# First-layer decays issued in mid-step through a spare PSUM bank, scans reordered; taps, squares and weight buffers changed in the third layer

## The chip, the core and the metric

The kernel runs on one core of a Trainium2 chip. Five engines work from their own queues, each in order: TensorE (PE, with its weight loads shown apart as PEld), VectorE (DVE), ScalarE (ACT), GpSimd (POOL) and SyncE (SP), which here issues all DMAs. The metric is the device time of one execution in microseconds (us), lower is better; the median of three runs of the kernel before is 7789.27 us.

## What is computed

A batch of 8 images of 384 channels and 32 x 32 pixels goes through four residual layers, each of the form `x = x + layer(group_norm(x))`, all in float32. Layers 0 and 2 are selective scans over the 1024 pixels of an image, with 768 inner channels `d` and 16 states `n` each; layer 2 adds a layer norm ahead of it and an MLP behind it. Layer 1 is a 1x1 convolution, an 8x8 patch filter in the frequency domain, a 3x3 depthwise convolution and a gate. Layer 3 is a 3x3 depthwise convolution. The core of layers 0 and 2:

```
def step(h, inp):
    dt_t, B_t, C_t, u_t = inp
    dA = jnp.exp(dt_t[..., None] * A)
    h = dA * h + (dt_t * u_t)[..., None] * B_t[:, None, :]
    y = jnp.einsum('bdn,bn->bd', h, C_t)
    return (h, y)
...
y = jnp.swapaxes(ys, 0, 1) + u * D
y = y * jax.nn.silu(z)
return y @ out_proj_w.T
```

## The kernel before, in words

**Tiling.** Each of the two scan layers is cut into 16 chunks (8 images, two halves of T = 512 pixels). A chunk is 24 steps (`QUADS`: six blocks of 128 inner channels, four sub-blocks each), so the main loop (lines 1015 to 1045) has 768 steps `t`. A step covers 32 inner channels x 16 states as four tiles of 128 x 512, j = 0 to 3. Steps 0 to 383 are layer 0 and steps 384 to 767 are layer 2.

**One step.** `begin` (line 610) loads dt*u for the step, repeated over the states, into a tile `g` (four tiles wide, four buffers), three steps ahead. `times` (line 619) multiplies `g` by B on POOL, two instructions of 128 x 1024, for step t+1. `decay` (line 627) spreads dt over the states by four matmuls of 32 rows into four PSUM banks `dAs[0..3]`, and ACT takes the exponentials in place. `scan` (line 637) runs four DVE scans, j = 0, 1, 2, 3. For j = 0 and 1 the result goes back into the bank and DVE multiplies it by C into `g` (line 654). For j = 2 and 3 it goes into `g`, and POOL multiplies both by C in one instruction (line 660). In the first half of an image, DVE copies keep the last column as `carry`. `gather` (line 664) sums over the states by matmuls into a bank `y`, one step later. At the end of a block of 128 channels it adds u*D (in layer 0 with a diagonal matrix `w_D`, loaded at the start by `load_diagonal`; in layer 2 on DVE) and multiplies by silu(z).

**Order.** It is written out by hand: the order of the calls is the order in each engine's queue. In the loop: `times(t+1)`, `scan(t)`, some job work (`jobs.step(t, 2.0)`, up to about 2 us of TensorE work), `gather(t-1)`, `begin(t+3)`, the rest of the job work (`jobs.step(t)`), and last `decay(t+1)`. In this text the two portions of job work are called J1 and J2.

**Jobs.** All else is cut into pieces by generators, and `Jobs` (line 90 on) puts them into the steps: `front` (loads, norms, input projection, the dt tiles), `gates` (z), `finish` (output projection; the MLP in layer 2), `layer1`, `layer3` and `measure` (group statistics). Each step grants a room of TensorE and DVE work (`ROOM`: 5.2 and 3.0 in layer 0, 6.4 and 3.0 in layer 2). Jobs go by due time, and `jobs.until` runs them at once where the loop can't go on without them. So work that was put off comes in a burst inside one step.

**PSUM.** Eight banks: four for the decays, one for `y`, and three (`NBANK`) that all jobs share in turn through `ps_tile` (line 179) and `pipe` (line 189). `live["ps"]` counts those in use; a job that finds none yields `WAIT`.

**The other places that the change touches.** `step_dt` (line 566) makes one dt tile per block: softplus with a scratch tile `spm` (two buffers, which `measure` and `layer_norm` use too, guarded by the flag `live["spm"]`), then dt*u into its own tile `du` (two buffers), which is spilled to DRAM. `layer_norm` (line 460, layer 2) squares a 128 x 512 tile on ACT and sums it on PE, three times in turn, through two buffers. `depthwise` (line 364) makes a diagonal matrix per tap on ACT and accumulates nine matmuls per tile; `layer3` (line 970) calls it for six tiles of 128 x 512 per image, then adds x on DVE into a single buffer `acc` and writes it out. `weights` (line 873) streams the MLP's weights from DRAM in pieces of 384 KB through four buffers `mw`.

```
        jobs.begin(ROOM["turn" if n == B * NCH else s["pre"]])
        jobs.step(t, 2.0)
        if t > 0:
            p, q = steps[t - 1]
            gather(p, q)
...
            begin(p, q)
        jobs.step(t)
        if t + 1 < total:
            decay(*steps[t + 1])
```

## Time and profile before

| what | value |
|---|---|
| median of 3 runs | 7789.27 us (7788.77 to 7790.12) |
| profiled execution, own time | 7774.96 us |
| its span on the core | 7773.2 us |
| mean granted TensorE clock | 0.922 of full speed |
| first scan starts at | 95.1 us |
| layer 0, steps 0 to 383 | 95.1 to 3552.3 us, 9.00 us a step |
| chunks 16 and 17 (the turn to layer 2) | 3552.3 to 4123.8 us |
| chunks 18 to 31 (layer 2, 336 steps) | 4123.8 to 7587.8 us, 10.31 us a step |
| tail after the last scan | 7587.8 to 7773.2 us |

Busy times are unions of the instructions' spans. A line of a group reads: source line, engine, operation, output<-inputs, shape, count | busy us, mean ns of one | idle time of that engine just before them, with what ended it. Helpers record for many callers: line 177 is every matmul, line 241 every activation, line 85 every metered DVE operation. A float32 matmul appears as two records, so the counts of PE are twice those of the program. In the timeline a line has the start, the duration, the engine and the instructions merged into it, with the idle time before the first of them in brackets.

### The profile page before, as it was taken

To read this page: it belongs to the slowest core of one execution; us is meant where nothing else is said; L and a number is where in the kernel's file an instruction comes from. 1 tells how busy PE (TensorE), PEld (TensorE's weight loads), DVE (VectorE), ACT (ScalarE), POOL (GpSimd) and SP (SyncE) were. 2 spreads that over 40 slices of the span, in tenths; PEclk is the share of its full clock that TensorE was granted. 3 is DMA by queue.
4 is the path that set the end of the run, shared out by engine and by line. 5 is a ranking of instruction groups with operands and counts; after the bars stand their busy time and mean duration, and the time that the engine had idled before them with its cause. 6 is when DMAs were issued, how large, how long until landed. Compare 5 with 4: busy or idle time off the path is not lost. (4 is left out here: it accounts for less than half of the span.)

```text
span 7773.2 us, 76689 instructions
## 1 busy us (share of the span) xinstructions
PE 7244.1 (93%) x25762; PEld 3001.0 (39%) x25762; DVE 5787.0 (74%) x7350; ACT 4034.0 (52%) x6980; POOL 5638.8 (73%) x2710
## 2 busy tenths in 40 slices
PE   7989999999999999999999989999999999999998
PEld 2223333333333333333334434444444444444445
DVE  5988788888777878778746765767777677776871
ACT  4445555554554555455545544555555555555543
POOL 5888878788787878778646764767767677676770
PEclk8888889999888999988899999999999999999999
DMA  5666556556565646556536654666656666565662
GB/s 141 141 151 144 138 134 142 136 135 150 127 146 127 141 120 148 128 139 146 129 78 167 174 135 120 165 156 172 165 150 174 155 170 164 149 164 146 171 168 67
DMA packets 288919, 1122.50 MB, mean 144 GB/s; under 512 B 37386, under 2 KB 90970, under 8 KB 190220
## 3 DMA queue, kind: packets, MB, share of 16 engines
q1 hardware_dynamic: 288524, 1117.59, 58.4%
q8 instruction: 204, 3.34, 0.2%
q14 instruction: 191, 1.56, 0.1%
HBM read 1041.96 MB, written 75.50 MB: 144 GB/s over the span
## 5 line engine op out<-in xcount | busy, mean ns | idle before, releaser
L623 POOL TENSOR_TENSOR g<-g,bc 128x1024 f32<-128x1024 f32 x1536 | 3586.8, 2358 | 197.2 <-DMA g<-dud 181.2
L660 POOL TENSOR_TENSOR g<-g,bc 128x1024 f32<-128x1024 f32 x768 | 1806.2, 2352 | 1441.1 <-DVE carry L656 806.6
L241 ACT ACTIVATE dA<-dA,w_A 128x512 f32<-128x512 f32 x3072 | 1860.7, 662 | 1543.3 <-PE dA L177 1530.1
L177 PE MATMUL dA<-dt,selr 32*128 32x512 f32 x6144 | 1573.3, 677 | 70.6 <-DVE g L654 61.9
L643 DVE TENSOR_TENSOR_SCAN dA<-dA,carry,g 128x512 f32<-128x512 f32 x768 | 986.6, 1285 | 616.0 <-issue 275.6
L643 DVE TENSOR_TENSOR_SCAN dA<-dA,g 128x512 f32<-128x512 f32 x768 | 940.6, 1225 | 477.5 <-issue 167.7
L654 DVE TENSOR_TENSOR g<-dA,bc 128x512 f32<-128x512 f32 x1536 | 1053.9, 686 | 29.8 <-DVE dA L643 0.5
L177 PE MATMUL y<-g,sely 128*32 128x512 f32 x6144 | 934.1, 637 | 43.0 <-POOL g L660 37.5
L643 DVE TENSOR_TENSOR_SCAN g<-dA,carry,g 128x512 f32<-128x512 f32 x768 | 940.6, 1267 | 0.0
L643 DVE TENSOR_TENSOR_SCAN g<-dA,g 128x512 f32<-128x512 f32 x768 | 893.3, 1204 | 0.0
L177 PEld LDWEIGHTS dA<-dt,selr 32*128 32x128 f32 x6144 | 470.2, 191 | 984.4 <-DVE g L643 517.3
L177 PE MATMUL ps_dn<-h,mw 128*128 128x256 f32 x2304 | 573.9, 401 | 75.3 <-DMA mw<-in_l_mlp_w 58.6
L177 PE MATMUL ps_up<-t,mw 128*128 128x256 f32 x2304 | 566.8, 394 | 59.0 <-DMA mw<-in_l_mlp_w 44.2
L177 PE MATMUL ps_z<-xf,w_in 128*128 128x512 f32 x1152 | 586.1, 649 | 27.3 <-DVE dt L85 23.6
L177 PE MATMUL ps_in<-xf,w_in 128*128 128x512 f32 x1152 | 566.9, 633 | 27.3 <-DVE u L85 25.5
L177 PE MATMUL ps_dw<-tp,diag 96*96 96x512 f32 x1152 | 572.8, 638 | 15.2 <-ACT diag L241 15.2
L177 PE MATMUL ps_out<-u,w_out 128*128 128x512 f32 x1152 | 543.7, 619 | 10.2 <-DVE x L85 10.2
L177 PEld LDWEIGHTS ps_dn<-h,mw 128*128 128x128 f32 x2304 | 439.5, 197 | 277.0 <-issue 118.8
L177 PEld LDWEIGHTS ps_up<-t,mw 128*128 128x128 f32 x2304 | 425.8, 192 | 268.4 <-issue 148.9
L177 PE MATMUL ps_dw<-xp,diag 128*128 128x512 f32 x864 | 407.5, 622 | 42.2 <-ACT diag L241 40.9
L241 ACT ACTIVATE u<-ps_in,w_vec 128x512 f32<-128x512 f32 x192 | 149.4, 778 | 484.2 <-PE ps_in L177 484.2
L177 PEld LDWEIGHTS y<-g,sely 128*32 128x32 f32 x6144 | 134.2, 111 | 648.5 <-issue 461.1
(99 smaller groups left out, 6463.1 us busy)
## 6 DMA issues: line engine op xcount, KB each, us to landing
g<-dud SPq DMA_DIRECT2D x768, 1024.0 KB, 7.1
mw<-in_l_mlp_w SPq DMA_DIRECT2D x384, 384.0 KB, 7.4
dud<-du SPq DMA_DIRECT2D x768, 64.0 KB, 1.7
xk<-in_x SPq DMA_DIRECT2D x48, 256.0 KB, 4.2
xf<-in_x SPq DMA_DIRECT2D x16, 768.0 KB, 8.4
x<-in_x SPq DMA_DIRECT2D x16, 768.0 KB, 8.5
x_mid<-x SPq DMA_DIRECT2D x16, 768.0 KB, 4.6
xk<-x_mid SPq DMA_DIRECT2D x48, 256.0 KB, 5.0
```

The lines of the kernel that those rows point to most:

```text
L177: nc.tensor.matmul(out_, lhsT, rhs, start=start, stop=stop)
L241: nc.scalar.activation(out_, in_, func, **kw)
L623: nc.gpsimd.tensor_mul(g, g, s["bc"][:, 0, :].unsqueeze(1).to_broadcast([P, 2, T]))
L643: nc.vector.tensor_tensor_scan(dAs[j] if j < own else g[:, j, :], dAs[j], g[:, j, :], 0.0 if s["c"] == 0 else carry[:, q : q + 1], ALU.mul ...
L654: nc.vector.tensor_mul(g[:, j, :], dAs[j], s["bc"][:, 1, :])
L660: nc.gpsimd.tensor_mul(g, g, s["bc"][:, 1, :].unsqueeze(1).to_broadcast([P, 4 - own, T]))
```

## The change

**In layer 0** the four scans of a step go in the order 2, 3, 0, 1 (`ORDER`), and POOL's multiplication of tiles 2 and 3 by C is queued once they are done. `decay(t+1)` moves ahead of J2, and its exponentials are issued in the order 2, 3, 0. The fourth (j = 1, `decay_last`) stays behind J2 and is written into another bank, `b2`, which the jobs therefore lose while layer 0 runs: they have two banks, and get `b2` back after the last scan of layer 0. The diagonal of D is made by ACT from the identity, block by block, instead of loaded.

**In layer 2** the order of scans and exponentials is 2, 3, 0, 1 as well; all four exponentials stay in place, and `decay(t+1)` stays at the end of the step. Everywhere `times` multiplies the upper half of `g` first.

**In layers 2 and 3**, three of the nine taps of layer 3 go from TensorE to POOL: per tile three multiplications by a per-channel weight (`tap`) and three additions (`acc`, beginning with x), and the DVE addition takes `acc` for x. `layer_norm` makes all three squares first, in three buffers, then the three matmuls. MLP weights have five buffers for four. `spm` has three buffers for two and also takes dt*u (`du` is gone), and its flag now tells who holds it.

```
+OWN = 2
+ORDER = (2, 3, 0, 1)
...
-    psg = ctx.enter_context(tc.tile_pool(name="psg", bufs=NBANK, space=PSUM))
+    psg = ctx.enter_context(tc.tile_pool(name="psg", bufs=1, space=PSUM))
...
+    live = {"dt": 0, "x": 0, "spm": None, "banks": ["b0", "b1"]}
...
+    def bank(name):
+        tag = live["banks"].pop(0)
+        ps = psg.tile([P, 512], F32, tag=tag, name=name)
+        held[id(ps)] = ps, tag
+        return ps
+    def ps_done(ps):
+        live["banks"].append(held.pop(id(ps))[1])
...
         while live["spm"]:
             yield WAIT
+        live["spm"] = "squares"
+        sq = [wk.tile([P, T], F32, tag="spm", name="sq", bufs=3) for _ in range(KC)]
+        for k in range(KC):
+            act(sq[k], xn[:, k, :], AF.Square)
+        yield NEXT
         ps = yield from ps_tile("ps_lv")
         for k in range(KC):
-            sq = wk.tile([P, T], F32, tag="spm", name="sq", bufs=2)
-            act(sq, xn[:, k, :], AF.Square)
-            mm(ps, ln_mean, sq, start=k == 0, stop=k == KC - 1)
+            mm(ps, ln_mean, sq[k], start=k == 0, stop=k == KC - 1)
...
-                v = got["du"] = wk.tile([P, T], F32, tag="du", name="du", bufs=2)
-                nc.gpsimd.tensor_mul(v, s["dt"][d], u[d])
+                nc.gpsimd.tensor_mul(got["m"], s["dt"][d], u[d])
...
-        for j in (0, 2):
+        for j in (2, 0):
             g = s["g", i][:, j : j + 2, :]
...
     def decay(s, i):
         k, sub = QUADS[i]
         for j in range(4):
             rows = slice(32 * j, 32 * (j + 1))
             mm(dAs[j], selr[rows, sub, :], s["dt"][k][rows, :])
...
-        for j in range(4):
-            act(dAs[j], dAs[j], AF.Exp, scale=s["w"]["A"][:, 4 * i + j : 4 * i + j + 1])
+        s["dA"] = list(dAs)
+        for j in ORDER:
+            if j != ORDER[-1] or s["pre"] == "l2_":
+                act(dAs[j], dAs[j], AF.Exp, scale=s["w"]["A"][:, 4 * i + j : 4 * i + j + 1])
+
+    def decay_last(s, i):
+        if s["pre"] == "l0_":
+            j = ORDER[-1]
+            s["dA"][j] = psg.tile([P, T], F32, tag="b2", name="dAx")
+            act(s["dA"][j], dAs[j], AF.Exp, scale=s["w"]["A"][:, 4 * i + j : 4 * i + j + 1])
...
+        dA = s["dA"]
-        for j in range(4):
+        for j in ORDER:
...
+            elif j == 3:
+                if s["c"] < NCH - 1:
+                    nc.vector.tensor_copy(
+                        carry[:, 4 * i + OWN : 4 * i + 4].unsqueeze(2), g[:, OWN:4, T - 1 : T]
+                    )
+                r = g[:, OWN:4, :]
+                nc.gpsimd.tensor_mul(
+                    r, r, s["bc"][:, 1, :].unsqueeze(1).to_broadcast([P, 4 - OWN, T])
+                )
...
+        if sub == NSUB - 2 and s["pre"] == "l0_":
+            s["D", k] = wk.tile([P, P], F32, tag="D", name="D")
+            act(s["D", k], eye, AF.Copy, scale=s["w"]["vec"][:, k, 4:5])
...
-                w = p2.tile([P, NFH, P], F32, tag="mw", name="mw", bufs=4)
+                w = p2.tile([P, NFH, P], F32, tag="mw", name="mw", bufs=5)
...
+                acc = p2.tile([P, T], F32, tag="acc", name="acc")
+                so_far = x[hf][:, k, :]
+                for t in range(3):
+                    tap = p2.tile([P, T], F32, tag="tap", name="tap")
+                    nc.gpsimd.tensor_scalar_mul(_img(tap), window(0, t), dw3[:, k, t : t + 1])
+                    nc.gpsimd.tensor_add(acc, tap, so_far)
+                    so_far = acc
+
                 def take(ps):
-                    acc = p2.tile([P, T], F32, tag="acc", name="acc")
-                    vector.tensor_add(acc, ps, x[hf][:, k, :])
+                    vector.tensor_add(acc, ps, acc)
                     nc.sync.dma_start(out[b, k * P : (k + 1) * P, rows], acc)

-                yield from depthwise(p2, P, [(dw3[:, k, :], window, take)])
+                yield from depthwise(p2, P, [(dw3[:, k, :], window, take)], 3)
...
         scan(s, i)
+        if t == total // 2 - 1:
+            live["banks"].append("b2")
         jobs.begin(ROOM["turn" if n == B * NCH else s["pre"]])
         jobs.step(t, 2.0)
...
+        nxt = steps[t + 1] if t + 1 < total else None
+        if nxt and nxt[0]["pre"] == "l0_":
+            decay(*nxt)
         jobs.step(t)
-        if t + 1 < total:
-            decay(*steps[t + 1])
+        if nxt and nxt[0]["pre"] == "l2_":
+            decay(*nxt)
+        if nxt:
+            decay_last(*nxt)
```

## The prediction

> **What bounds the kernel now.** I read the page first, then the busy times by stage, then groups by form, then the timeline. The page says that TensorE is the fullest engine, but not at full clock.
>
> ```profile
> PE 7244.1 (93%) x25762; PEld 3001.0 (39%) x25762; DVE 5787.0 (74%) x7350; ACT 4034.0 (52%) x6980; POOL 5638.8 (73%) x2710
> PEclk8888889999888999988899999999999999999999
> ```
>
> By stage (length; busy PE, PEld, DVE, ACT, POOL; clock), layer 0, then layer 2:
>
> ```profile
> 95.10:3552.30 3457.20, 3265.68 (x10785) 1132.42 (x10786) 2839.63 (x3567) 1816.76 (x3220) 2814.81 (x1349) 0.90 0.58 138
> ...
> 4123.80:7587.80 3464.00, 3225.17 (x12705) 1547.98 (x12704) 2540.83 (x3249) 1841.81 (x3050) 2455.78 (x1174) 0.96 0.63 160
> ```
>
> Layer 0 takes 9.00 us a step; DVE works 2839.6/384 = 7.39 of it and POOL 7.33. DVE's idle 617.6 us is what there is to win. The timeline of one step shows how it arises:
>
> ```profile
> 2021.09 2.45 DVE L643 TENSOR_TENSOR_SCAN g<-dA,carry,g 128x512 f32<-128x512 f32 x2
> ...
> 2023.32 2.84 PE L177 MATMUL ps_out<-u,w_out 128*128 128x512 f32 x6
> ...
> 2026.09 1.14 PE L177 MATMUL dA<-dt,selr 32*128 32x512 f32 x8
> ...
> 2027.25 2.40 ACT L241 ACTIVATE dA<-dA,w_A 128x512 f32<-128x512 f32 x4 [4.22 <-PE dA L177]
> ...
> 2028.00 1.29 DVE L643 TENSOR_TENSOR_SCAN dA<-dA,carry,g 128x512 f32<-128x512 f32 x1 [4.46 <-POOL g L660]
> ```
>
> DVE is done with the scans at E = 2023.54. PE is still on a job matmul and reaches the decays at P = 2026.09. The next scan starts at 2028.00, P + 1.91. (The bracket names POOL, but the first exponential, ending at 2027.9, is what came last.) I took P, E and the next start S from the trace for every step. S - P is never under 1.91. In layer 0, 182 steps have S - P below 1.97, so the arrival of the decays set them: 312 us of DVE idle. The other scan starts lost 106 us and the rest of DVE about 200. In 245 of 384 steps PE came before E and waited for the last scan. So the ring DVE - PE - ACT sets layer 0, with job work of uneven size in it. In layer 2, 228 of 383 steps are set by the decays (548 us); there TensorE's work is the bound.
>
> **What the Trainium skill says.** TensorE: Matmul & The Clock Gate, Part 2, LDWEIGHTS step: matmuls stay in program order, only weight loads are pulled ahead. The trace agrees: the decays above started only after `ps_out`. The same page, Part 1: the clock is full or half, by how busy TensorE was. The trace agrees with 0.43 us against 0.86 from one weight load of `ps_z` to the next, and 0.90 granted in layer 0. GPSIMD Engine Reference, 3.1: an operation with one input can reach 1.8 cycles an element, 769 ns for 512; no run here shows one. For two inputs the trace has 1272 ns (`du`).
>
> **The change part by part.** Prices, with layer norm and weight waits:
>
> ```profile
> L177 PE MATMUL ps_lv<-sq,ln_mean 128*128 128x512 f32 x96 | 72.4, 915 | 40.2 <-ACT sq L241 40.2
> L177 PE MATMUL ps_ln<-xf,ln_mean 128*128 128x512 f32 x96 | 55.6, 725 | 7.9 <-ACT gnm L241 5.7 <-ACT xf L241 2.2
> L177 PE MATMUL ps_dn<-h,mw 128*128 128x256 f32 x2304 | 573.9, 401 | 75.3 <-DMA mw<-in_l_mlp_w 58.6 <-ACT h L241 11.2 <-DVE dA L643 2.6
> L177 PE MATMUL ps_up<-t,mw 128*128 128x256 f32 x2304 | 566.8, 394 | 59.0 <-DMA mw<-in_l_mlp_w 44.2 <-DVE dt L85 5.5 <-ACT h L241 5.4
> L583 POOL TENSOR_TENSOR du<-dt,u 128x512 f32<-128x512 f32 x192 | 244.2, 1272 | 157.2 <-DVE dt L85 153.0 <-DMA dud<-du 4.2
> L241 ACT ACTIVATE diag<-eye,vec 128x128 f32<-128x128 f32 x432 | 160.0, 400 | 161.0 <-PE ps_dw L177 160.7
> ```
>
> (1) Layer 0, ring. In the new order the decays wait for tile 0's multiplication; only scan and multiplication of tile 1 are still to come then, 1.24 + 0.69 = 1.93 us on DVE. Decay to scan is 1.91, so the next scan can follow at once even if PE waited. PE leaves the decays 1.93 us earlier in the step, and is as much earlier at the next ones. Cutting each of the 182 gaps by at most 1.93 removes about 220 us of 312. Of the 106 us others, where POOL's factors were often late, I take 25: POOL starts on tiles 2 and 3 before the last two scans and is some 4 us earlier. I count 200 + 25 = -225. Both ends: 0 if another wait takes over, -365 if DVE idle falls to 250.
>
> (2) Against it, in layer 0. J2 now lies behind the decays, so DVE jobs fed by J2 may arrive after E. The built order has 58 such steps; from the end of the decays (1.1 us of matmuls and 0.3 of handing over), J2's matmuls at 0.43 a record, less the 1.93 and other DVE work, they sum to +45. Two banks: matmuls whose bank was evicted after less than 1 us of other PE work rise from 5 to 55 for ACT (0.6 us eviction) and from 0 to 24 for DVE. ACT: 50 x 0.4 = 20; DVE: 24 x 1 = 24, half hidden by the slack that (1) leaves; +35. Moved past J2 on ACT are three exponentials, 2.0 us; J2's evictions wait for matmuls behind the decays anyway: 0. The fourth exponential waits for the end of tile 1's multiplication, with J1's evictions of the next step queued behind it; it takes 0.66 and is needed 2.45 + 1.93 = 4.4 us into the next step: 0, and 0.7 a step if not. SP: `begin` stays ahead of the decays. D's diagonals: 96 x 400 ns = 38 us of ACT, 53% busy, at least a step ahead: 0, or 38 uncovered. Layer 0: -225 + 80 = -145.
>
> (3) Layer 2, taps. TensorE loses 144 matmuls, 3 x 2 x 0.43 = 2.57 us for each of 48 tiles. POOL gains 3 x (0.8 + 1.27) = 6.2 us a tile, 7.6 if the one-input operation costs as much as the two-input one; I take the page's. In the built order 25 tiles stand alone in a step, 17 in six bursts, 6 in the tail. Alone: 25 x 2.57 = 64, of which 60% (228 of 383) lies on the path: -38. POOL's addition waits for `acc` to be written out (2.0 us to landing), and C's and B's factors queue behind it: 1.5 us for gather or scan, 25 x 1.5 = +38 (0 to 7.6 each). In the bursts a tile is now addition 1.27, two pairs 4.1, DVE 0.7, DMA 2.0 and hand-overs, 8.4 us, where nine taps took 7.7: 0. Tail: 6 x 1 = +6.
>
> (4) Squares: `ps_lv` occupies 112.6 us where the equal `ps_ln` occupies 63.5; 49 x 0.6 = -29. Weights: waits of 58.6 + 44.2 = 103; a fifth buffer takes a third, x 0.6 = -21 (0 to -62).
>
> (5) Layer 2, order of scans with the decays at the end. The last bank free is now tile 1's, second of the four matmuls, with tile 2's exponential behind it; so a scan starts no sooner than E + 1.9, where before it could follow E. Where PE waited (171 steps), filling S - E up to 1.9 gives 82 us; 70%: +57 (0 to 100). The earlier POOL gives -30 of the 116 us that the other scan starts lost. The change in burst sizes at the turn (PE work between decays 103 and 56 us before, 98 and 43 after): -18.
>
> Sum: -145 - 38 + 38 + 6 - 29 - 21 + 57 - 30 - 18 = -180. Profiled execution 7774.96 - 180 = 7595. The median of the runs is 14.3 us above it, so 7609: **7610 us**, 0.977 of before.
>
> **Rivals.** *The ring opens fully in layer 0*: DVE idle there falls to 250. For it: PE's own need is only 5.36 us between decays (built order, 0.43 a record) + 1.07 for the decays at full clock, under DVE's 7.39. Against it: uneven steps remain. 7789 - 365 - 35 = 7390.
>
> *Two banks take the gain back*: the 24 DVE evictions stand behind whole scans, 24 x 4.5 = 108, and 55 ACT ones cost 0.8, 44: 152 against 145. The change then doesn't do what it is for, and the rest gives 7789 - 35 = 7755. Against it: only 79 of the job matmuls' waits are that short.
>
> *POOL becomes the bound in layer 2* (slower): each tile's 7.6 us stands whole in front of the factors, since its addition waits for the previous `acc`, and DVE and PE stop for it. 48 x 7.6 = 365 instead of about 50: 7610 + 315 = 7920. It decides from about 5 us a tile (180/48 + 1). For it: one buffer, and a strided read not priced here. Against it: 10.31 - 7.31 = 3.0 us of POOL idle a step, and half a step of lead.
>
> **How the numbers follow.** Forecast 0.55 (7540 to 7690), open ring 0.18 (7300 to 7500), banks 0.15 (7690 to 7810), POOL 0.12 (7800 to 8000). The range 7380 to 7780 leaves out 8 in 100 below and 12 above. A measurement of this kernel can tell about 0.2%, 16 us. Faster: 0.55 + 0.18 + 0.12 of the bank case = 0.85; same 0.04; slower 0.11.
>
> **What would show it.** Layer 0 below 8.7 us a step with the same DVE work and less idle before its first scan; S - P still 1.91. `ps_lv` near `ps_ln`. In layer 2 more DVE idle put down to ACT before the first scan. A one-input POOL line of 0.8 us. Wrong, if layer 0 keeps its length while matmuls wait for evictions, or if POOL's tap lines are followed by scans that wait for POOL.

## The result, and the profile after

The changed kernel takes 8218.42 us (median of 4 runs, 8206.54 to 8234.36) where the kernel before takes 7789.02 (4 runs): a ratio of 1.0553, 95% interval 1.0534 to 1.0571. It is 5.5% slower; 2.3% faster was forecast. The profiled execution took 8206.54 us, its span is 8204.7, its mean TensorE clock 0.896.

| stretch of the profiled execution, us | before | after |
|---|---|---|
| layer 0, steps 0 to 383 | 3457 | 3634 |
| chunks 16 and 17 (the turn) | 572 | 595 |
| chunks 18 to 31 (layer 2) | 3464 | 3702 |
| tail after the last scan | 185 | 181 |

Both layers lose, 177 and 238 us. The page's busy times and its row of granted clocks, for the changed kernel:

```profile
PE 6930.0 (84%) x25474; PEld 2884.6 (35%) x25474; DVE 5909.5 (72%) x7350; ACT 3987.8 (49%) x6932; POOL 6042.2 (74%) x2998
...
PEclk8788888989899988989889989899999999998998
```

The busy times by stage, layer 0 and then layer 2 (length; busy PE, PEld, DVE, ACT, POOL with counts; clock, DMA share, GB/s):

```profile
92.50:3726.70 3634.20, 2981.49 (x10803) 1038.54 (x10804) 2916.23 (x3567) 1835.66 (x3327) 2817.34 (x1351) 0.88 0.56 132
4321.50:8023.60 3702.10, 3236.14 (x12503) 1548.43 (x12502) 2582.20 (x3250) 1797.96 (x2947) 2798.75 (x1420) 0.92 0.59 150
```

In layer 0 the stage grows by 177 us while TensorE's busy time falls by 284. That fall is mostly a matter of counting. In the old order the four matmuls of a step's decays waited for scans 2 and 3 in the middle of their group, and such a wait lies inside the group's busy time; in the new order the wait stands ahead of the group, for the multiplication of a scan's result by C. The groups of layer 0 alone, before and after:

```profile
L177 PE MATMUL dA<-dt,selr 32*128 32x512 f32 x3071 | 908.8, 698 | 60.5 <-DVE g L654 54.5
```

```profile
L176 PE MATMUL dA<-dt,selr 32*128 32x512 f32 x3072 | 520.9, 744 | 404.7 <-DVE g L671 404.2
```

Busy and idle together are 969 us before and 926 after. So TensorE's new waits are not in sum at the decays: its idle time ahead of all other matmuls of layer 0 rises from 140 to 256 us. What lengthens the layer is read better from DVE.

I sorted DVE's idle time in the trace by what came after it: the first scan of a step, or a job's operation. "Copies" is the busy time of the 128x2 copy that saves the carry of tiles 2 and 3.

| us | before, layer 0 | after, layer 0 | before, layer 2 | after, layer 2 |
|---|---|---|---|---|
| idle ahead of the first scan | 429 | 291 | 606 | 670 |
| idle ahead of job operations | 165 | 396 | 292 | 426 |
| copies | 76 | 145 | 38 | 73 |

In layer 0 the first line improves by 138, as the change meant, and the other two take back 231 and 69. The sum, +162, is nearly the 177 that the layer lost, but it tells where DVE waits and not yet why. In layer 2 all three lines rise, by 64 + 134 + 35 = 233 of 238.

### The profile page after: what moved, and what is told of

Read it like the earlier page. It is cut to its first block, busy times and chain, and to the rows that moved or that the text cites. A ratio compares the mean times of both kernels' runs of the same rounds, so it can differ in the third digit from the quotient of the medians.

```text
span 8204.7 us, 76917 instructions
## 1 busy us (share of the span) xinstructions
PE 6930.0 (84%) x25474; PEld 2884.6 (35%) x25474; DVE 5909.5 (72%) x7350; ACT 3987.8 (49%) x6932; POOL 6042.2 (74%) x2998
## 5 line engine op out<-in xcount | busy, mean ns | idle before, releaser
L246 ACT ACTIVATE dA<-dA,w_A 128x512 f32<-128x512 f32 x2688 | 1617.2, 660 | 2378.1 <-PE dA L176 2349.6
L176 PE MATMUL dA<-dt,selr 32*128 32x512 f32 x6144 | 1172.1, 719 | 574.1 <-DVE g L671 572.7
L671 DVE TENSOR_TENSOR g<-dA,bc 128x512 f32<-128x512 f32 x1152 | 790.8, 686 | 19.7
L176 PEld LDWEIGHTS dA<-dt,selr 32*128 32x128 f32 x6144 | 322.3, 202 | 1281.0 <-DVE g L671 1015.7
L660 DVE TENSOR_TENSOR_SCAN dA<-dA,carry,g 128x512 f32<-128x512 f32 x576 | 732.4, 1271 | 0.0
L176 PE MATMUL ps_in<-xf,w_in 128*128 128x512 f32 x1152 | 613.7, 682 | 110.8 <-DVE u L84 105.2
L660 DVE TENSOR_TENSOR_SCAN dA<-dA,g 128x512 f32<-128x512 f32 x576 | 706.0, 1226 | 1.1 <-issue 0.5
L84 DVE SCALAR_TENSOR_TENSOR u<-ps_in,w_vec,u 128x511 f32<-128x511 f32 (+1 forms) x384 | 285.3, 747 | 276.4 <-ACT xt L246 189.9
L176 PEld LDWEIGHTS ps_in<-xf,w_in 128*128 128x128 f32 x1152 | 236.5, 217 | 483.3 <-issue 425.4
L589 POOL TENSOR_TENSOR spm<-dt,u 128x512 f32<-128x512 f32 x192 | 243.9, 1270 | 175.3 <-DVE dt L84 175.3
```

The lines of the kernel that those rows point to most:

```text
L84: return call(out_, *args, **kw)
L176: nc.tensor.matmul(out_, lhsT, rhs, start=start, stop=stop)
L246: nc.scalar.activation(out_, in_, func, **kw)
L589: nc.gpsimd.tensor_mul(got["m"], s["dt"][d], u[d])
L660: nc.vector.tensor_tensor_scan(dA[j] if j < OWN else g[:, j, :], dA[j], g[:, j, :], 0.0 if s["c"] == 0 else carry[:, q : q + 1], ALU.mult, ...
L671: nc.vector.tensor_mul(g[:, j, :], dA[j], s["bc"][:, 1, :])
```

## The experiments

Times are medians. Each has its ratio to the kernel before, run beside it on the same chip, with its 95% interval; differences between experiments are differences of these ratios times 7785 us, good to some 30 us. Stage lengths come from one profiled execution each. No kernel leaves out any of the computation.

**First round: which edit?** The first theory put layer 0's loss on the decays in mid-step with their lost bank, and layer 2's on POOL's taps. The rival: the new order, or the rest.

e1: layer 0's decays at the end, in place, with three banks; all else as changed.

```
-        if nxt and nxt[0]["pre"] == "l0_":
-            decay(*nxt)
         jobs.step(t)
-        if nxt and nxt[0]["pre"] == "l2_":
+        if nxt:
             decay(*nxt)
```

> The changed kernel, with layer 0 treated like layer 2: decays at the end of the step, all four exponentials in place, three banks for jobs; the new order of scans and all else kept. Theory A (the decays in mid-step with two banks cost layer 0 its 177 us, since job matmuls and job DVE operations now wait for each other across the scans): job matmuls that wait for a DVE operation behind the scans of their own step fall from 131 to 34, layer 0 falls from 3634 us by 177, less what the order 2, 3, 0, 1 costs with the decays at the end (0 to 136): 8040 to 8180 us in all. Theory B (the order of scans itself, through the small carry copies and the POOL overlap, costs layer 0): layer 0 stays near 3600, 8190 to 8230.

Measured 8240.39, ratio 1.0579 (1.0541 to 1.0618). Layer 0 stays at 3663: DVE's idle ahead of job operations falls from 396 to 118, its idle ahead of the first scan rises from 291 to 679. The time is above both ranges, and layer 0 does as theory B has it. So the lost bank and the mid-step are not alone at fault; without them the new order loses as much. The copies of layer 0 are short again (67 us for 145), so the order's cost does not come through them.

e2: the old order in layer 2 (`for j in ORDER` becomes `range(4)` there; POOL still multiplies the upper half of `g` by B first).

> The changed kernel with scans and exponentials of layer 2 in the old order 0, 1, 2, 3; layer 0 as changed. Theory A (with the decays at the end of the step, the scan that is first now needs a decay behind the last bank to come free, 1.9 us after the last scan): layer 2 falls by 60 to 100 us, 8120 to 8160 in all, and the shortest waits from last scan to next first scan drop from 1.98 to about 0.5 us. Theory B (POOL's earlier start in the new order is worth as much as the wait costs): 8200 to 8240.

Measured 8181.73, 1.0501 (1.0456 to 1.0547). That is between the two theories. Layer 2 proper stays at 3710; the turn falls from 595 to 567.

e3: all nine taps on TensorE.

> The changed kernel with all nine taps of layer 3 on TensorE again. Theory A (POOL's taps cost about what they save; layer 2's loss comes from elsewhere): 8180 to 8260 us, DVE's wait for the tap result about 160 us as before. Theory B (POOL is the bound in layer 2, 8.5 us a tile with the measured 1566 ns for a tap): layer 2 falls by 150 us or more, 8070 or less.

Measured 8142.2, 1.0453 (1.0415 to 1.0491); layer 2 at 3637. That is 65 of its 238, and the time is 78 us less by the ratios: between the two theories.

e4: e1, e3 and the old order together. What stays are squares ahead of their sums, five weight buffers, dt*u in the shared buffer, D by ScalarE, and the list of free banks.

> The changed kernel without its three large edits: decays at the end in both layers, old order, nine taps on TensorE, three banks. What is left is the squares made ahead, the fifth weight buffer, spm in three buffers and D made by ACT. Theory A (the squares' extra step boundary shifts the input projection of layer 2 to steps where two of three banks are held by half-done tiles, so that job matmuls waiting behind scans rise from 74 to 123): layer 0 near 3457 us, layer 2 longer than before by 50 to 140 us, 7810 to 7930 in all. Theory B (these edits help, as forecast): 7720 to 7760.

Measured 7952.0, 1.021 (1.0171 to 1.0249); layer 0 at 3500, layer 2 at 3610. The edits that I had forecast as a gain of 50 cost 165, a little more than theory A has. I had not priced what they do to the packing of the jobs. The trace of the changed kernel shows it in layer 2 (timeline: start, duration, engine and instructions, idle time in brackets):

```profile
5751.42 2.84 PE L176 MATMUL ps_in<-xf,w_in 128*128 128x512 f32 x6
...
5754.30 0.78 ACT L246 ACTIVATE u<-ps_in,w_vec 128x512 f32<-128x512 f32 x1 [0.38 <-PE ps_in L176]
...
5756.56 1.28 DVE L660 TENSOR_TENSOR_SCAN dA<-dA,carry,g 128x512 f32<-128x512 f32 x1
...
5758.49 1.52 DVE L84 SCALAR_TENSOR_TENSOR u<-ps_in,w_vec,u 128x511 f32<-128x511 f32 x2
5760.16 5.46 PE L176 MATMUL ps_in<-xf,w_in 128*128 128x512 f32 x6 [4.91 <-DVE u L84]
...
5766.53 1.53 DVE L84 SCALAR_TENSOR_TENSOR u<-ps_in,w_vec,u 128x511 f32<-128x511 f32 x2 [6.51 <-ACT xt L246]
5767.98 2.45 DVE L660 TENSOR_TENSOR_SCAN g<-dA,carry,g 128x512 f32<-128x512 f32 x2
```

By the built order, both input projections of this step use one bank, since a depthwise tile and a half-done up-projection hold the others. The first is evicted by DVE, whose `u` stands behind all four scans, to 5760.01. TensorE idles 4.91 us for it, then runs at half clock (0.50 granted from 5760.16 to 5765.62; 5.46 us for six records, 2.84 in the first line), and DVE idles 6.51 for the second. In the built order I counted the job matmuls that wait for a DVE job operation issued in their own step, and so behind its scans: 24 in layer 0 and 74 in layer 2 before; 131 and 127 in the changed kernel; 34 and 123 in e4.

**Second round: order, banks, squares, copies.**

e5: the kernel before with the new order alone, decays at the end, three banks in turn.

```
-        for j in range(4):
+        for j in (2, 3, 0, 1):
...
-        for j in range(4):
+        for j in (2, 3, 0, 1):
             q = 4 * i + j
...
+            elif j == 3:
...
+                nc.gpsimd.tensor_mul(
```

> The kernel before, with the order of scans and exponentials 2, 3, 0, 1, POOL's multiplication by C queued after scan 3 and the upper half of g multiplied by B first; decays at the end of the step, three banks in turn, nothing else. Theory (the order costs by itself, in both layers, because the bank that comes free last is tile 1's and the first exponentials stand behind the matmul that fills it): layer 0 goes from 3457 us to 3570-3640, layer 2 from 3464 to 3510-3570, the time from 7789 to 7930-8060. The copies of the carry from g double, 120 to 220 us. Rival (the order is harmless, and what layer 0 lost with the decays at the end came from the handling of the job banks): both layers within 30 us of before, 7750-7830.

Measured 7968.73, 1.0219 (1.0184 to 1.0254): layer 0 3645, turn 603, layer 2 3454. The theory holds for layer 0 (+188) and falls for layer 2 (-10, where 46 to 106 was expected). The copies in layer 0 did not grow (70 us); all together took 143.

e6: e4 with the banks in fixed turn, as before.

```
-    psg = ctx.enter_context(tc.tile_pool(name="psg", bufs=1, space=PSUM))
+    psg = ctx.enter_context(tc.tile_pool(name="psg", bufs=3, space=PSUM))
...
-        ps = psg.tile([P, 512], F32, tag=tag, name=name)
+        ps = psg.tile([P, 512], F32, tag="ps", name=name)
```

> e4 (7952 us) with one thing put back: the job banks are taken in fixed turn as before, instead of the one that was given back first. In the built order the job matmuls that wait for a DVE operation behind the scans of their own step fall from 34 to 24 in layer 0 (24 before) and from 123 to 87 in layer 2 (74 before). Theory (bank choice is what costs): layer 0 falls from 3500 to about 3460, layer 2 from 3610 to 3510-3540, the time to 7810-7860. Rival (squares ahead, or dt*u in the shared buffer, is what costs): it stays at 7910-7960.

Measured 7870.55, 1.0096 (1.006 to 1.0131): layer 0 3469, layer 2 3563. Between theory and rival: the choice of bank is about half of what e4 lost.

e7: e6 without the break between squares and sums.

```
             act(sq[k], xn[:, k, :], AF.Square)
-        yield NEXT
         ps = yield from ps_tile("ps_lv")
```

> e6 with the squares and their three matmuls left in one piece of job work (the break between them taken out), so that layer 2's packing is that of before and the count of waits is 74 again. What is left of the change is three squares ahead of three matmuls, five weight buffers, dt*u in the shared buffers and D made by ACT. Theory (the break shifts the packing of layer 2 so that the two input projections of a step share one bank): 50-100 us less than e6, and 7730-7790, at or below the kernel before, by what squares and weights were forecast to give (-50). Rival (the break is harmless and the shared buffer costs): within 15 us of e6.

Measured 7698.57, 0.9874 (0.9842 to 0.9907): layer 2 3368, and the fastest yet. One `yield NEXT` costs 173 us, well over the 50 to 100 of the theory. The groups of input projection and squares, first e6, then e7, show both sides:

```profile
L176 PE MATMUL ps_in<-xf,w_in 128*128 128x512 f32 x1152 | 596.3, 660 | 94.6 <-DVE u L84 88.8 <-ACT dA L246 4.1 <-ACT xf L246 1.7
...
L176 PE MATMUL ps_lv<-sq,ln_mean 128*128 128x512 f32 x96 | 45.5, 610 | 0.0
```

```profile
L176 PE MATMUL ps_in<-xf,w_in 128*128 128x512 f32 x1152 | 567.5, 633 | 27.1 <-DVE u L84 25.4 <-ACT xf L246 1.7
...
L176 PE MATMUL ps_lv<-sq,ln_mean 128*128 128x512 f32 x96 | 68.6, 872 | 39.4 <-ACT sq L246 39.4
```

The break wins the 39.4 us wait of the sums and 23 us of their busy time, and moves everything behind it by a step. In layer 2 DVE idles 204 us less in e7 than in e6. The largest piece is the wait for ScalarE's `xt` ahead of `u`, which is the wait of 6.51 us in the timeline above: 86 us in e6, 8 in e7.

e8: the changed kernel with the 128x2 copy made as two of 128x1.

```
-    nc.vector.tensor_copy(
-        carry[:, 4 * i + OWN : 4 * i + 4].unsqueeze(2), g[:, OWN:4, T - 1 : T]
-    )
+    for m in range(OWN, 4):
+        nc.vector.tensor_copy(carry[:, 4 * i + m : 4 * i + m + 1], g[:, m, T - 1 : T])
```

> The changed kernel, with the one copy of 128x2 that saves the carry of tiles 2 and 3 made as two copies of 128x1. Theory (a copy of two elements from SBUF to SBUF needs the port that POOL holds, and so waits for POOL's running instruction, while one element doesn't): the two copies take 100-160 ns each in place of 594 for the one, carry from g falls from 228 to about 100 us, and the time by 40-110, to 8110-8180. Rival (the copy is long because it waits for the scan's last write, or for another reason that has no part in the number of elements): the first copy stays near 500 ns, carry at 250 us or more, the time at 8210-8270.

Measured 8098.1, 1.0389 (1.0355 to 1.0424), a little more than expected: layer 0 at 3568. One such copy in the timeline of the changed kernel, with POOL's instructions beside it:

```profile
2452.95 4.67 POOL L631 TENSOR_TENSOR g<-g,bc 128x1024 f32<-128x1024 f32 x2
...
2456.81 0.83 DVE L674 COPY carry<-g 128x2 f32<-128x2 f32 x1
```

The group of these copies in the changed kernel, then in e8:

```profile
L674 DVE COPY carry<-g 128x2 f32<-128x2 f32 x384 | 228.2, 594 | 13.1
```

```profile
L675 DVE COPY carry<-g 128x1 f32<-128x1 f32 x768 | 104.0, 141 | 0.0
```

The long copy ends at 2457.64, with POOL's multiplications (2457.62). That is the rule: of the 384 copies in the changed kernel 145 took over 200 ns, and 144 of these ended within 30 ns of the end of a POOL instruction. In e8 none of the 768 took over 156 ns, though POOL worked through the whole of 323.

**Third round: are they the cause inside the changed kernel?**

e9: the changed kernel with three job banks in layer 0. Tiles 2, 3 and 0 are decayed in mid-step, tile 1 in place behind J2.

```
-        for j in range(4):
+        for j in (0, 2, 3) if mid else range(4):
...
-            s["dA"][j] = psg.tile([P, T], F32, tag="b2", name="dAx")
+            mm(dAs[j], selr[rows, sub, :], s["dt"][k][rows, :])
```

> The changed kernel, with the jobs' third bank kept in layer 0: in mid-step go the decays of tiles 2, 3 and 0 alone, and tile 1's matmul and exponential, in place, stand behind J2. In the built order the job matmuls of layer 0 that wait for a DVE operation behind the scans of their own step fall from 131 to 28 (24 in the kernel before). Theory (what eats the gain of the mid-step decays in layer 0 is the bank that the jobs lose): layer 0 falls from 3634 to 3440-3530 us, the time from 8218 to 8020-8115; with one job bank more, DVE's waits ahead of job operations fall from 387 to 200-260. Rival (the place of J2 behind the decays makes the jobs late, whatever the banks): layer 0 stays above 3590, the time above 8170.

Measured 8213.69, 1.0572 (1.0551 to 1.0593), layer 0 at 3648. The theory falls: the job waits in the built order are gone (28 for 131), and the time has not moved. DVE's idle ahead of job operations stays at 358. The bank's return was paid for by putting tile 1's matmul behind J2, so the run says that this exchange gains nothing, not that a bank is worth nothing by itself; layer 0's loss is there with three banks as with two.

e10: the changed kernel without the break, a job taking the free bank whose use began longest ago.

```
-        tag = live["banks"].pop(0)
+        tag = min(live["banks"], key=lambda b: used.get(b, 0))
```

> The changed kernel with two edits that act on the packing alone: a job takes the free bank whose last use began longest ago, and the squares and their matmuls stay in one piece of job work. Taps on POOL, scan order, mid-step decays and two banks in layer 0 are kept. In the built order the waits of job matmuls behind the scans of their own step fall from 127 to 61 in layer 2, and stay in layer 0 (131 to 137). Theory (layer 2's loss is packing of the jobs into banks, not POOL and not the order): layer 2 falls from 3702 to 3480-3540, layer 0 keeps 3610-3660, the time falls to 7990-8070. Rival (taps on POOL and the new order hold layer 2 up): layer 2 stays above 3620, the time above 8130.

Measured 8232.73, 1.0592 (1.0571 to 1.0614), layer 2 at 3660, layer 0 at 3694. By its numbers the rival wins, but the test is spoiled: TensorE's wait of `ps_in` for `u` fell from 82 to 10 us in layer 2, while one of `ps_up` for ScalarE's `h` rose from 20 to 91, which no kernel with banks in turn has.

e11: e7 with the copies split.

> e7 (7699 us) with the carry from g copied in two pieces of 128x1, as in e8. Theory (each copy takes 141 ns and DVE's time is on the path where the scans set the pace): the carry from g falls from 130 to 108 us in all, that of layer 0 from 68 to 54; with POOL's port left alone the time falls by 5-40, to 7660-7695. Rival (it is hidden, since in the old order the copies seldom wait for POOL): 7690-7710.

Measured 7675.23, 0.9877 (0.9857 to 0.9897). Against e7's 0.9874 there is no gain to be told: in the old order the copies wait less for POOL (130 us in e7, 108 split).

e12: e11 with layer 0 in the new order and e9's mid-step.

> e11 with layer 0 in the new order and its decays of tiles 2, 3 and 0 in mid-step, tile 1's behind J2, three job banks in turn; layer 2 stays in the old order. Theory (the ring is what sets layer 0, and without the loss of a bank, without the long copies and with the banks in turn the mid-step decays give what was forecast): layer 0 falls from about 3450 to 3250-3380, the time to 7460-7610. Rival (job operations that arrive late take most of it): layer 0 stays within 40 us of 3450, the time at 7640-7710.

Measured 7813.58, 1.0056 (1.004 to 1.0072), layer 0 at 3596, above both ranges. The mid-step has three banks, short copies and banks in turn, and still loses. The timeline of e12 in layer 0 shows how:

```profile
1066.32 0.68 DVE L675 TENSOR_TENSOR g<-dA,bc 128x512 f32<-128x512 f32 x1
...
1067.06 1.13 PE L176 MATMUL dA<-dt,selr 32*128 32x512 f32 x6 [0.59 <-DVE g L675]
...
1068.12 2.84 PE L176 MATMUL ps_in<-xf,w_in 128*128 128x512 f32 x6
...
1068.23 1.82 ACT L246 ACTIVATE dA<-dA,w_A 128x512 f32<-128x512 f32 x3 [4.06 <-PE dA L176]
1068.25 0.68 DVE L675 TENSOR_TENSOR g<-dA,bc 128x512 f32<-128x512 f32 x1
...
1071.00 0.78 ACT L246 ACTIVATE u<-ps_in,w_vec 128x512 f32<-128x512 f32 x1 [0.95 <-PE ps_in L176]
1071.81 1.53 DVE L84 SCALAR_TENSOR_TENSOR u<-ps_in,w_vec,u 128x511 f32<-128x511 f32 x2 [2.28 <-ACT u L246]
...
1073.26 3.65 DVE L84 BATCH_NORM_STATS2 st<-x 128x6 f32<-128x512 f32 x6
...
1077.08 2.29 DVE L664 TENSOR_TENSOR_SCAN g<-dA,g 128x512 f32<-128x512 f32 x2
```

TensorE waits for tile 0's multiplication and does the decays at 1067.06. J2's `ps_in` follows, to 1070.96, then ScalarE's `u`, then DVE's. DVE has been done with the scans since 1068.93 and with a short addition since 1069.53, and idles 2.28 us. The exponentials are ready at 1070.05, but 5.3 us of job operations stand ahead of the scan, to 1077.08. Before, J2 ran under the scans.

**Fourth round: one clean base.**

e13: e12 with more job work ahead of the decays.

```
-        jobs.step(t, 2.0)
+        jobs.step(t, 3.4 if s["pre"] == "l0_" else 2.0)
```

> e12 (layer 0 3596 us) with the first portion of job work, J1, granted 3.4 us of TensorE work in layer 0 instead of 2.0, so that less of it stands behind the mid-step decays. In e12 TensorE waits 280 us in layer 0 for tile 0's multiplication (181 times 1.5 us), and then does J2, whose results DVE awaits behind its scans (u, dt, gate, u*z: about 300 us of DVE idle, 115 in the kernel before). Theory (J2 behind the decays comes too late for DVE, and TensorE is idle ahead of them): TensorE's wait falls under 150 us, DVE's idle ahead of job operations under 200, layer 0 to 3440-3530, the time to 7660-7750. Rival (the ring itself has no gain to give: what DVE wins on job operations it loses ahead of its first scan, since the decays come later): layer 0 stays at 3570-3620.

Measured 7746.77, 0.9954 (0.9939 to 0.9969), layer 0 at 3537. Between the two: the idle ahead of job operations falls from 356 to 207, that ahead of the first scan rises from 396 to 489. TensorE's wait for tile 0 falls only to 240. Late job results are a cause; taking them away gives back 59 us of layer 0 and not the 73 more that would reach e11.

e14: e9 with banks in turn and no break.

> e9 (8214 us, layer 2 3710) with three job banks in fixed turn and the squares in one piece with their matmuls: the changed kernel with its taps, orders and mid-step decays, but the packing of before. e10 was to show the same for layer 2, but the choice of bank that it made brought waits of its own (up-projection for ScalarE, 91 us, which neither the kernel before nor e7 has). In the built order the waits of job matmuls behind the scans of their own step are 64 in layer 2 (74 in the kernel before, 127 in the changed one). Theory (packing is what layer 2 lost): layer 2 at 3420-3540, the time at 7930-8050. Rival (taps on POOL and the new order hold layer 2 up by themselves): layer 2 above 3620, the time above 8120.

Measured 8055.92, 1.0352 (1.033 to 1.0373), layer 2 at 3559, between the two theories. Packing is 151 of layer 2's loss in the changed kernel; it was 242 in e4 to e7.

e15: the kernel before with five weight buffers (D by ScalarE makes room).

> The kernel before with five weight buffers in place of four, and D's diagonal made by ScalarE (which frees the room for them); nothing else. Theory (the waits for weights, 103 us of TensorE, are what e7 won in layer 2, and the squares gave nothing): layer 2 falls from 3464 to 3370-3410, layer 0 stays within 15 us of 3457, the time at 7690-7730. Rival (e7's gain comes from squares or from dt*u in the shared buffer): layer 2 at 3440 or more, the time at 7750-7790. My forecast for the fifth buffer was 21 us.

Measured 7719.96, 0.9912 (0.9884 to 0.994), layer 2 at 3399. The theory holds for layer 2: most of e7's gain is the fifth buffer. Layer 0 is at 3480, 22 us longer than before where the theory allowed 15; whether D by ScalarE costs that can't be told from one profile each. The waits for weights, 58.6 and 44.2 us before, in e15:

```profile
L177 PE MATMUL ps_up<-t,mw 128*128 128x256 f32 x2304 | 569.1, 397 | 44.2 <-DVE dt L85 27.6 <-DMA mw<-in_l_mlp_w 12.1 <-ACT h L241 3.6
L177 PE MATMUL ps_dn<-h,mw 128*128 128x256 f32 x2304 | 563.3, 398 | 28.5 <-DMA mw<-in_l_mlp_w 14.3 <-ACT h L241 11.2 <-ACT gnm L241 1.8
```

e16: e11 with the taps on POOL.

> e11 (7675 us, layer 2 3379) with three of layer 3's nine taps on POOL, as in the change; nothing else. My forecast for the taps was 0 in the chunks of layer 2 (-38 and +38) and +6 in the tail. Theory now (a tap takes POOL 1.57 us where 0.8 was taken, so a tile's chain is 8.5 us; DVE's addition, the factors and the carry copies stand behind it): layer 2 up by 50-110 us, the time at 7725-7790. Rival (the forecast holds, and layer 2 of the changed kernel lost by packing and order alone): within 20 us of e11.

Measured 7870.76, 1.0121 (1.0102 to 1.0139), layer 2 at 3542: even the theory's range was too low. The groups of e11 and e16 show what stands behind a tile's chain on POOL beside DVE's addition, namely the gathers that need POOL's product with C:

```profile
L176 PE MATMUL y<-g,sely 128*32 128x512 f32 x6144 | 940.1, 635 | 74.3 <-POOL g L676 71.9 <-DVE u L701 1.9
```

```profile
L176 PE MATMUL y<-g,sely 128*32 128x512 f32 x6144 | 972.2, 636 | 195.8 <-POOL g L676 194.4 <-DVE u L701 1.2
```

Of layer 2's +164, DVE's idle ahead of job operations makes 113 (261 to 374), that ahead of the first scan 48 (564 to 612). Of the 113, 100 are ahead of the addition that ends a tile of layer 3.

e17: e12 with layer 0's decays back at the end.

> e12 (7814 us, layer 0 3596) with layer 0's decays back at the end of the step; the new order in layer 0, split carry copies and all else as there. So e11 to e17 is the order, e17 to e12 the place of the decays, e12 to e13 the share of work ahead of them. Theory (the order costs layer 0 because the last bank comes free with tile 1's multiplication and the first exponential stands behind its matmul; mid-step wins part of that back): layer 0 at 3610-3650, the time at 7820-7880. Rival (with the copies split the order costs little, and the mid-step itself is the loss): layer 0 under 3540, the time under 7760.

Measured 7839.52, 1.0072 (1.005 to 1.0095), layer 0 at 3609: at the lower edge of the theory. The order costs 145 us of layer 0. The mid-step wins back 13: it moves 262 us out of the wait for the first scan (658 to 396) and puts 231 into job waits (125 to 356), with smaller ones besides. The groups of the first scans in layer 0 (through 3600 us), first e11 (tile 0), then e17 (tile 2):

```profile
L659 DVE TENSOR_TENSOR_SCAN dA<-dA,carry,g 128x512 f32<-128x512 f32 x384 | 493.2, 1284 | 248.7 <-issue 127.0 <-POOL g L630 40.7 <-ACT dA L246 38.6
L659 DVE TENSOR_TENSOR_SCAN dA<-dA,g 128x512 f32<-128x512 f32 x396 | 485.1, 1225 | 220.5 <-ACT dA L246 84.7 <-issue 61.8 <-POOL g L630 27.9
```

```profile
L659 DVE TENSOR_TENSOR_SCAN g<-dA,g 128x512 f32<-128x512 f32 x384 | 448.4, 1209 | 312.5 <-issue 222.8 <-POOL g L630 47.5 <-ACT dA L246 26.2
L659 DVE TENSOR_TENSOR_SCAN g<-dA,carry,g 128x512 f32<-128x512 f32 x362 | 444.6, 1270 | 328.0 <-issue 141.4 <-ACT dA L246 125.3 <-POOL g L630 46.6
```

"Issue", where the profile names no releaser, grows; in fact the step's first exponential comes last. In e17, 645 us of the idle time ahead of first scans end within 0.15 us of its end, which leaves some ten. The time from the last scan or multiplication of a step to its next first scan is 0.32 us at its 5th and 1.33 at its 25th percentile in e11; in e17 it is 1.98 at both. The upper half of `g` comes first in layer 2 of e17 too, where e11 has the lower one; layer 2 is as long (3384 and 3379).

e18: e11 with the new order in chunks 18 to 31 alone.

> e11 with the new order of scans, exponentials and halves of g in chunks 18 to 31 of layer 2 alone, decays at the end. My forecast for the order there was +57 (a bubble of up to 1.9 us wherever TensorE waits for the scans) and -30 (POOL starts earlier). Theory (in layer 2 the two cancel, as e5 showed with -10): the time within 25 us of e11's 7675. Rival (the bubble counts in full, and POOL was no limit): 7700-7760.

Measured 7713.13, 0.9912 (0.9892 to 0.9932), layer 2 at 3398, turn at 586: +27 us by the ratios (38 by the medians), over the theory's 25 and at the low end of the rival's range. That is the forecast's net of +27 for the order in layer 2, but the error is as large as the number.

**The sum.** Edit by edit, from the pair that comes nearest to differing in it alone:

| edit | from | us |
|---|---|---|
| new order, layer 0 | e11, e17 | +152 |
| decays in mid-step, layer 0 | e17, e12 | -12 |
| the third bank lost, tile 1's decay ahead of J2 | e9, changed | -15 |
| new order, layer 2 | e11, e18 | +27 |
| taps on POOL | e11, e16 | +190 |
| break behind the squares | e7, e6 | +173 |
| first bank given back | e6, e4 | +89 |
| fifth weight buffer, with D by ScalarE | before, e15 | -69 |
| 128x2 copies in the changed kernel | e8, changed | +128 |

They add up to 663 where the change cost 430. The parts overlap, and most of them come from kernels other than the changed one. Inside the changed kernel the taps are 78 us (e3) in place of 190, and the break and the banks together 171 (e9 to e14) in place of 262; with these two the sum is 460, which is 430 within the error. The three squares ahead and dt*u in the shared buffer have no row; e15 to e7, which adds them, is -30, at the edge of what can be told.

## Why the prediction was wrong, step by step

**(1), the ring, -225: mis-sized, and with (2) it decided layer 0.** The idle time ahead of first scans fell by 138 us in the changed kernel, and by some 70 on the clean base (e11 to e12). "The next scan can follow at once even if PE waited" was right: in the 185 steps of the changed kernel's layer 0 in which TensorE waited for tile 0's multiplication, that idle time averages 0.25 us. What failed is the rest of the step. The 182 gaps that the decays' arrival set in the kernel before fell from 312 to 166 us in the same steps of the changed kernel, by 146 and not 220: TensorE was not "as much earlier at the next ones". The 106 us of the other 201 steps did not fall by 25; they are 116. And the sum set the mid-step against the kernel before and left out what the new order itself costs. In the old order the banks of tiles 0 and 1 come free long ahead of the last scan, and 25% of the steps start within 1.33 us of it. In the new order with the decays at the end, none starts under 1.97; that is 145 us of layer 0 (e17). Most of it sits in those 201 steps: 127 us of idle time ahead of their first scans in e11, 283 in e17, 140 with the mid-step back (e12). I had priced this bubble for layer 2, (5), but not for layer 0, where the mid-step has to earn it back first. It earns 13 (e12), 72 with J1 at 3.4 us (e13), and never reaches the old order.

**(2), late J2 operations, +45: mis-sized about five times.** DVE's idle ahead of job operations rose by 231, with three banks on a clean base just the same (e12 against e17). My count took only DVE operations that read what TensorE had written. It left out those fed through ScalarE (`u`, `xt`, the softplus), for which I wrote that the exponentials ahead of J2's evictions cost 0. By what the trace says ended them, waits for ScalarE rose from 108 to 257 us and those for TensorE from 18 to 108 (changed kernel), so the part that I did count was twice its price as well. On DVE everything queued behind a late operation is late as well, the next scan last of all.

**(2), two banks, +35: no sign of it.** e9 gave the bank back, with tile 1's decay behind J2 in exchange, and won nothing; e12 has three banks and loses. So the rival that put layer 0's loss there was wrong, though the bank's own price was not measured.

**(3), taps, 0 and +6 in the tail: measured +190 on the clean base (e16), +78 in the changed kernel (e3).** The tap was priced at 0.8 us; it took 1.57:

```profile
L1012 POOL TENSOR_SCALAR tap<-xp,vec 128x512 f32<-128x512 f32 x144 | 225.5, 1566 | 43.0 <-ACT xp L246 31.9
...
L1013 POOL TENSOR_TENSOR acc<-tap,x 128x512 f32<-128x512 f32 x48 | 60.8, 1268 | 92.3 <-DMA out<-acc 81.8 <-DVE g L660 6.4 <-DVE g L671 2.6
...
L84 DVE TENSOR_TENSOR acc<-ps_dw,acc 128x512 f32<-128x512 f32 x48 | 33.0, 687 | 259.4 <-POOL acc L1013 234.0 <-PE ps_dw L176 25.4
```

These are groups of the changed kernel. A tile is 3 x (1.57 + 1.27) = 8.5 us of POOL, and DVE waits 234 us for its end. That is not all new: the same addition waited 231.5 us for TensorE's ninth matmul in the kernel before, so POOL took over a wait and added 28 us to it here, 98 in e16 (231.5 in e11, 329.9 there). The other part is the gathers' wait for POOL's product with C, up by 122 in e16. The 38 us that TensorE's lighter work was to give don't show. 190/48 is 4.0 us a tile: near the point of about 5 from which I let the rival "POOL becomes the bound in layer 2" decide. That rival, at 7920, was the nearest to the measured time, but by luck: taps are less than half of the loss on either base. How much of the tile's cost is the single `acc` (81.8 us of waiting for its write) was not tried.

**(4), squares -29, weights -21.** With the break the squares won what was said, `ps_lv` at 623 ns a record for 915 and no wait left. But the break was not costed as what it is, a shift of all later job work by a step. It cost 173 (e6 and e7). The fifth buffer was undervalued: -69, since the waits fell by 76 of 103 us, not by a third.

**(5), order in layer 2: right in size as far as can be told**, +27 net, measured +27 (e18). Layer 2 proper gives +20 there, -10 in e5 and -8 from e2, so the sign is open, and the +57 and -30 can't be told apart. The -18 at the turn failed: the turn grew by 23, and with the old order in layer 2 (e2) it is 27 shorter again.

**What the forecast didn't have at all**: the banks' new order, +89, and the copies, +128. The diff showed both, a list for a turn, and a copy that moved from behind all scans to between them. In layer 0 it took the mid-step as well to make the copies long: 145 us in the changed kernel, 67 and 70 with the decays at the end (e1, e5), 76 before.

What I can't settle is why e13 still is 73 us behind e11 in layer 0. An estimate from the trace of the kernel before, argued and not shown: per step of layer 0, the larger of TensorE's and DVE's busy time averages 8.65 us, and the step takes 9.00. With 1.13 us a step for the decays, so that their inner waits are not counted as work, it is 8.46. So of the 617 us of DVE idle that I took as what there is to win, only some 140 to 210 (384 x 0.35 or 0.54) could be won by placing work within its step; the rest would be the unevenness of the steps.

## What to carry to other kernels

Where queues are written by hand, a yield, a list of free banks or a place in the order has a price of its own: build the changed order and look which matmuls wait for an operation queued behind the long instructions of their step, ScalarE's hand-overs included. The count alone is no price: in e9 it fell from 131 to 28, and the time did not move. Price a new order at its own shortest gap before crediting what is meant to fill it. And try the edits alone: the best kernels here (e7 and e11, 0.987 and 0.988 of before) keep the fifth weight buffer, the squares in one piece and the banks in turn, and drop the order, the mid-step and the taps.

## What the runs showed of the hardware

A DVE copy of two elements from SBUF to SBUF took 594 ns on average in the changed kernel and 313 before, one of one element 141 (e8). The Trainium skill, page "SBUF — State Buffer", section "Who interferes with whom", says that a copy can enter a mode that takes the port pair shared with GpSimd, and that whoever comes second is blocked until the other's instruction ends. The traces agree: 144 of 145 long copies ended within 30 ns of a POOL instruction. Six of them took over 2.4 us, more than the 2.35 of one such instruction, so they did not get in at its end. I had not looked for it in so small an operation.

POOL's multiplication of 512 elements by a per-channel weight took 1566 ns where it read rows of the padded image; the figure of 769 ns in the Trainium skill, page "GPSIMD Engine Reference", section 3.1, is a best case that no run here came near.

TensorE's mean granted clock in layer 0 was 0.899 in e11 and 0.868 in e17, where its waits for DVE ahead of the decays went from 40 to 207, of 1.5 us on average. But e12 has 181 such waits of the same length at 0.897, so the waits alone don't tell the clock. Nor does the clock explain layer 0: e12 is 132 us longer there than e11 at the same clock. In layer 2 the clock fell from 0.96 before to 0.92 in the changed kernel, and what that cost by itself was not told apart.
